# A graph layer on one core: taking 22 self-loops per step out of the gathers

## The chip, the core and the metric

The kernel runs on one core of a Trainium2 chip. The metric is the device time of one execution in microseconds. Kernels are compared by the median of several runs; a profile is one further execution, with its own time.

## What is computed

The reference is one layer of a graph network on 50000 nodes with 128 features, with a residual and a layer norm:

```python
Xs = X[src]                                   # one row per edge, 1650000 edges
m_data = Xs @ W_data.T + b_data
m_ctrl = Xs @ W_control.T + b_control
msg = jnp.where((edge_types == 0)[:, None], m_data, m_ctrl)
agg = jax.ops.segment_sum(msg, dst, num_segments=X.shape[0])
out = relu(agg + (X @ W_self.T + b_self))
x = layernorm(x + out)
```

The edges are sorted by destination. They are 800000 random pairs in both directions, and one self-loop per node (src equal to dst). The sort is stable and the loops came last, so a node's loop is the last of its about 33 edges. Each edge has a type, 0 or 1, at random.

## The kernel before

The sum over the edges comes ahead of the weights. For each node the kernel sums the source rows of its edges of type 0 and of type 1 separately, and counts both; the weights and biases are then applied to the two sums and the counts.

**Blocks, steps, chunks.** The edge list is cut into 449 blocks of 3680 edges. A block has 28 chunks of 128 edges and one chunk of 96. It is worked on in four steps of seven chunks (the fourth has the 96 as well). A step's edges end in a window of W = 36 nodes, a block's in B = 128 nodes. Ten blocks are a group, whose edge data are loaded at once.

**Gathers.** For each chunk of 128 edges, `products` (L246) issues one indirect DMA from POOL: it fetches the 128 source rows of 512 bytes by a list of indices in SBUF into a buffer y, of which there are 70. The 96 rows of the last chunk come as single-row DMAs, half from SP's queue and half from ACT's (L234), into yx.

**Products.** TensorE multiplies each chunk's rows with a one-hot matrix (L249), which sends each row to its node's column of its type, and sums a step in PSUM (acc). The one-hot matrix of a block is one compare on VectorE (L198) of the edges' columns col_g with a row of numbers that lies in PSUM (num_ps). The counts are reductions of it (L208, L213) that TensorE puts into a third part of acc (L252).

**Sums.** VectorE adds each step's acc into a ring of three tiles, sums (L260), at the place of the step's window. ACT copies what the next block shares with this one (take_over, L265). `layer` (L270 to L273) multiplies with the weights on TensorE, `moments` and `store` (L278 to L293) do the residual, the norm and the store, one block later.

**Columns.** Once per group `columns` (L155 to L165) turns destinations and types of 128 x 290 edges into columns, and takes a least and a greatest value. These go into a flag at the end: where an edge falls out of its window, a general path recomputes everything. The flag stays zero with these inputs.

**Order.** The order is written out by hand. Each engine runs its instructions in program order. The loop runs over blocks b and steps q; the one-hot matrix, the counts and the single rows are made two blocks ahead (AHEAD). The lists of indices are used as they were loaded (tile idx_g), so the first gather waits for one load only. At the start of the run POOL's iota for num (L127) stands behind the first gathers in POOL's order, and VectorE's copy of it (L130), the clearing of sums (L145 to L147) and the computation of every block's first node from first_i (base, begin; L108 to L116) follow on VectorE.

Of the kernel before, what the change touches and what calls it, by code (L numbers as in the profile page):

```python
# [11 lines left out]
F32 = mybir.dt.float32  # L12
BF16 = mybir.dt.bfloat16
# [11 lines left out]
P = 128  # L25
# [6 lines left out]
R = 7  # L32
# [5 lines left out]
C1 = C + 1  # L38
BE = C * CH + X
NBLK = -(-E // BE)  # L40
# [6 lines left out]
GC = GB * C1  # L47
AHEAD = 2


# [17 lines left out]

def straight(ctx, tc, c, x, x_t, src_t, dst_t, etype_t, src_x, dst_first, out):

# [13 lines left out]
    ohp = ctx.enter_context(tc.tile_pool(name="ohp", bufs=AHEAD + 1))  # L84
    gat = ctx.enter_context(tc.tile_pool(name="gat", bufs=70))
    stp = ctx.enter_context(tc.tile_pool(name="stp", bufs=3))
    ps = ctx.enter_context(tc.tile_pool(name="ps", bufs=4, space=bass.MemoryType.PSUM))
    ps_o = ctx.enter_context(tc.tile_pool(name="ps_o", bufs=2, space=bass.MemoryType.PSUM))

    idx_g, d_g, t_g, one_g, col_g = {}, {}, {}, {}, {}  # L90
    stats = keep.tile([P, 2, GROUPS], F32, name="stats")

    def load_edges(g):
        t = eds.tile([1, GB * X], I32, name="one_g")
        nc.sync.dma_start(t, src_x[None, g * GB * X:(g + 1) * GB * X])
        one_g[g] = t
        for name, a, of in (("idx_g", src_t, idx_g), ("d_g", dst_t, d_g), ("t_g", etype_t, t_g)):
            t = eds.tile([P, GC], I32, name=name)
            nc.sync.dma_start(t, a[:, g * GC:(g + 1) * GC])
            of[g] = t  # L100

# [26 lines left out]
                   allow_small_or_imprecise_dtypes=True)  # L128
    num_ps = keep_ps.tile([P, 2 * W], F32, name="num_ps")
    nc.vector.tensor_copy(num_ps, num)  # L130

    to_row = keep.tile([P, 2, P], BF16, name="to_row")
    nc.vector.memset(to_row, 0.0)
# [10 lines left out]
    for t in sums:  # L144
        nc.vector.memset(t, 0.0)  # L145
        nc.vector.memset(t[0:3, 2, :], 1.0)
        nc.vector.memset(t[0:2, 2, :], 0.0)  # L147

    def columns(g):

        d, t = d_g.pop(g), t_g.pop(g)
        rel = eds.tile([P, GC], F32, name="rel")
        first = begin[:, g * GB:(g + 1) * GB, :]
        rel_b, d_b = (a.rearrange("p (b c) -> p b c", c=C1) for a in (rel, d))
        nc.vector.tensor_tensor(rel_b[:, :, :C].rearrange("p b (q r) -> p b q r", r=R),  # L155
                                d_b[:, :, :C].rearrange("p b (q r) -> p b q r", r=R),
                                first[:, :, :, None].to_broadcast([P, GB, Q, R]), op=ALU.subtract)
        nc.vector.tensor_tensor(rel_b[:, :, C:], d_b[:, :, C:], first[:, :, Q - 1:], op=ALU.subtract)
        col = eds.tile([P, GC], F32, name="col_g")
        nc.vector.tensor_scalar(col, t, 0.0, float(W), op0=ALU.not_equal, op1=ALU.mult)  # L160
        nc.vector.tensor_tensor(col, col, rel, op=ALU.add)
        chk = eds.tile([P, GC], F32, name="chk")
        nc.vector.scalar_tensor_tensor(chk, d, float(DST_PAD), rel, op0=ALU.is_lt, op1=ALU.mult)
        nc.vector.tensor_reduce(stats[:, 0, g:g + 1], chk, AX.X, ALU.min)
        nc.vector.tensor_reduce(stats[:, 1, g:g + 1], chk, AX.X, ALU.max)  # L165
        col_g[g] = col

# [5 lines left out]
    def steps_of(b):  # L173
        return [q for q in range(Q) if len(chunks_of(b, q))]

    ohs, cnts, ys, accs, xws, xTs, pos, hs, mvs, sds = {}, {}, {}, {}, {}, {}, {}, {}, {}, {}

# [12 lines left out]
    def onehot(b):  # L192
        g, i = divmod(b, GB)
        if i == 0:
            columns(g)
        n = C1 if b < NBLK - 1 else RCH
        oh = ohp.tile([P, C1, 2 * W], F32, name="oh")
        nc.vector.tensor_tensor(oh[:, :n, :], col_g[g][:, i * C1:i * C1 + n, None].to_broadcast([P, n, 2 * W]),  # L198
                                num_ps[:, None, :].to_broadcast([P, n, 2 * W]), op=ALU.is_equal)
        ohs[b] = oh  # L200
# [20 lines left out]
    def single_rows(b, q):  # L221

        if q == 0:
            ys[b] = stp.tile([X, D], F32, name="yx", bufs=AHEAD + 2)
        g, i = divmod(b, GB)
        both = []
        for j, (eng, dma) in enumerate(((SP, nc.sync), (ACT, nc.scalar))):
            at = j * SHARE + q * TURN
            _, nodes = nc.values_load_multi_w_load_instructions(  # L229
                one_g[g][0:1, i * X + at:i * X + at + TURN], engines=[eng], **RANGE)  # L230
            both.append([(dma, at + k, node) for k, node in enumerate(nodes)])
        for pair in zip(*both):
            for dma, row, node in pair:
                dma.dma_start(ys[b][row:row + 1, :], x[bass.ds(node, 1), :])  # L234

    def products(b, q):
        g, i = divmod(b, GB)
        acc = ps.tile([P, 3, W], F32, name="acc")
        ks = chunks_of(b, q)
        for k in ks:  # L240
            if k == C:
                r, y = X, ys.pop(b)
            else:
                r = LAST if b == NBLK - 1 and k == RCH - 1 else P
                y = gat.tile([P, D], F32, name="y")
                nc.gpsimd.indirect_dma_start(  # L246
                    out=y[:r], out_offset=None, in_=x,
                    in_offset=bass.IndirectOffsetOnAxis(ap=idx_g[g][:r, i * C1 + k:i * C1 + k + 1], axis=0))
            nc.tensor.matmul(acc[:, :2, :].rearrange("p t w -> p (t w)"), y[:r], ohs[b][:r, k, :],  # L249
                             start=k == ks[0], stop=k == ks[-1])  # L250
        for t in range(2):
            nc.tensor.matmul(acc[:, 2, :], to_row[:, t, :], cnts[b][:, q, t * W:(t + 1) * W],  # L252
                             start=t == 0, stop=t == 1)
        accs[b, q] = acc
# [39 lines left out]

    with tc.manual_schedule():
        for b in range(AHEAD):
            onehot(b)
            counts(b)
        for b in range(3):
            window(b)  # L300
        for b in range(AHEAD):
            for q in range(Q):
                single_rows(b, q)
        for b in range(NBLK + 1):
            if b + 3 < NBLK:
                window(b + 3)
            g, i = divmod(b, GB)
            if i == GB // 2 and g + 1 < GROUPS:
                load_edges(g + 1)
            if b > 0:  # L310
                add(b - 1, steps_of(b - 1)[-1])
                if b < NBLK:
                    take_over(b)
            qs = steps_of(b)
            for q in range(Q):
                if q in qs:
                    products(b, q)
                if q == 0 and b > 0:
                    layer(b - 1)
                if q in qs[:-1]:  # L320
                    add(b, q)
                if q == 0 and b > 0:
                    moments(b - 1)
                if q == 0 and b + AHEAD < NBLK:
                    onehot(b + AHEAD)
                if q == 1 and b > 0:
                    store(b - 1)
                if b + AHEAD < NBLK - 1:
                    single_rows(b + AHEAD, q)
                if q == 1 and b + AHEAD < NBLK:  # L330
                    counts(b + AHEAD)

# [3 lines left out]
    mm = keep.tile([P, 2], F32, name="mm")  # L336
    nc.vector.tensor_reduce(mm[:, 0:1], stats[:, 0, :], AX.X, ALU.min)
    nc.vector.tensor_reduce(mm[:, 1:2], stats[:, 1, :], AX.X, ALU.max)
    bad = keep.tile([P, 2], F32, name="bad")
    nc.vector.tensor_scalar(bad[:, 0:1], mm[:, 0:1], 0.0, None, op0=ALU.is_lt)  # L340
# [6 lines left out]
    pb = ps_o.tile([B, D], F32, name="po")  # L347
    nc.tensor.matmul(pb[:2, 0:1], bad, ones, start=True, stop=True)
    both = keep.tile([2, 1], F32, name="both")
    nc.vector.tensor_copy(both, pb[:2, 0:1])  # L350
    pc = ps_o.tile([B, D], F32, name="po")
    nc.tensor.matmul(pc[:1, 0:1], both, ones[:2, 0:1], start=True, stop=True)
    nc.vector.tensor_copy(gap[:, 2:3], pc[:1, 0:1])
# [227 lines left out]
def gnn_resnorm(  # L581
# [5 lines left out]
    dst_t: bass.AP,  # L587
    etype_t: bass.AP,
    src_x: bass.AP,
    dst_first: bass.AP,  # L590
# [37 lines left out]
    with ExitStack() as own:  # L628
        straight(own, tc, c, x, x_t, src_t, dst_t, etype_t, src_x, dst_first, out)
    found = nc.values_load(bad, min_val=0, max_val=4 * P,  # L630
                           skip_runtime_bounds_check_because="a count of at most 2 * P + 2")
    with tc.If(found > 0):
# [35 lines left out]
```

## Time and profile before

| what | value |
|---|---|
| time, median of 3 runs | 15709.57 us (15708.91 to 15711.14) |
| the profiled execution: its time | 15709.39 us |
| the profiled execution: span from first to last instruction | 15707.6 us |
| granted TensorE clock | 1.000 |
| busy: POOL / TensorE / VectorE / ACT | 76% / 62% / 24% / 2% |
| bytes moved by DMA | 971.47 MB, mean 62 GB/s |
| gathers | 12555 |
| single-row DMAs | 2 x 21504 |

A row of a group names line, engine, operation, output and inputs, and how often it ran; after the bar come the busy time in us and the mean of one in ns; after the second bar the time that the engine was idle just before these instructions, and what ended most of it. "issue" is idle time in which the engine waited for nothing that the profile shows. L249 counts two matmuls per chunk[...]. A two-input operation on VectorE is called TENSOR_TENSOR or SCALAR_TENSOR_TENSOR, one with a single tensor TENSOR_SCALAR, COPY or CAST.

### The profile page before, as it was taken

What the parts mean: (1) busy time and instruction counts of PE and PEld (TensorE: products, weight loads), DVE (VectorE), ACT (ScalarE), POOL (GpSimd) and SP (SyncE); (2) the same over time, 40 slices, a digit from 0 to 9 for tenths busy, and PEclk for the clock granted to TensorE, in tenths of its full rate; (3) what the DMA queues carried; (4) which work ended last, traced back from release to release, by engine and by line L of the source; (5) the groups of instructions that cost most, each with busy time, mean ns of one, the idle gap of its engine ahead of it and who ended that gap; (6) DMA issues with size and microseconds to landing.
All of it is one profiled execution on the core that took longest, in us unless ns stands there. A gap on an engine that the chain in (4) does not pass through costs nothing.

```text
span 15707.6 us, 248219 instructions
## 1 busy us (share of the span) xinstructions
PE 9719.2 (62%) x33193; PEld 7477.1 (48%) x33194; DVE 3846.6 (24%) x5740; ACT 365.0 (2%) x903; POOL 11860.3 (76%) x12563
## 2 busy tenths in 40 slices
PE   5666666666666666666666666666666666666666
PEld 4444444444444444444444444444444444444444
DVE  3222222222222222222222222222222222222222
ACT  0000000000000000000000000000000000000000
POOL 7777777777777777777777777777777777777777
DMA  2222222222222222222222222222222222222222
GB/s 65 62 62 62 62 63 62 62 62 62 62 62 62 63 62 62 62 62 62 62 62 63 62 62 62 62 62 62 62 63 62 62 62 62 62 62 62 63 62 58
DMA packets 703530, 971.47 MB, mean 62 GB/s; under 512 B 267712, under 2 KB 500803, under 8 KB 701856
## 3 DMA queue, kind: packets, MB, share of 16 engines
q0 software_dynamic: 401760, 823.58, 20.1%
q1 hardware_dynamic: 256650, 120.61, 2.9%
q10 hardware_dynamic: 43446, 11.29, 0.3%
q14 instruction: 1397, 11.44, 0.2%
q8 instruction: 277, 4.54, 0.1%
HBM read 924.99 MB, written 29.43 MB: 61 GB/s over the span
## 4 chain that ended last, share of the span: by engine, by line
DMA 39%; issue 37%; PE 14%; POOL 8%; ACTq 2%; DVE 0%; SPq 0%; POOLq 0%; ACT 0%; DVEq 0%
DMA y<-in_x,idx_g 38%; PE acc L249 9%; POOL y L246 8%; PE po L273 2%; PE po L271 1%; DMA yx<-in_x 1%; PE po L270 1%; ACTq L234 1%; ACTq L229 0%; PE acc L252 0%; SPq L234 0%; POOLq L246 0%; SPq L229 0%; DVE sums L260 0%; DVE st L280 0%
## 5 line engine op out<-in xcount | busy, mean ns | idle before, releaser
L246 POOL DMA_INDIRECT y<-in_x,idx_g x12555 | 11859.4, 945 | 3832.3 <-issue 2666.4
L249 PE MATMUL acc<-oh,y 128*128 128x72 f32 x25110 | 8397.3, 448 | 5957.2 <-DMA y<-in_x,idx_g 5852.6
L249 PEld LDWEIGHTS acc<-oh,y 128*128 128x128 f32 x25110 | 6240.9, 314 | 7996.6 <-DMA y<-in_x,idx_g 7247.8
L260 DVE TENSOR_TENSOR sums<-acc,sums 128x108 f32 x1794 | 486.0, 271 | 10835.0 <-PE acc L252 9773.4
L208 DVE TENSOR_REDUCE cnt<-oh 128x216 bf16<-128x1512 f32 (+1 forms) x449 | 1268.5, 2825 | 0.1
L198 DVE TENSOR_TENSOR oh<-col_g,num_ps 128x2088 f32<-128x2088 f32 (+1 forms) x449 | 1030.7, 2296 | 0.0
L252 PEld LDWEIGHTS <-to_row 128*128 128x128 bf16 x3588 | 654.4, 198 | 0.0
L273 PE MATMUL po<-wmsgT,sums 128*128 128x128 f32 x1796 | 548.7, 461 | 0.0
L213 DVE TENSOR_REDUCE cnt<-oh 128x72 bf16<-128x576 f32 (+1 forms) x449 | 526.1, 1172 | 0.0
L265 ACT COPY sums<-sums 128x384 f32 x448 | 229.4, 512 | 11662.5 <-DMA yx<-in_x 11590.1
L252 PE MATMUL acc<-cnt,to_row 128*128 128x36 bf16 x3588 | 480.1, 217 | 0.0
L273 PEld LDWEIGHTS po<-wmsgT,sums 128*128 128x128 f32 x1796 | 416.3, 322 | 100.7 <-issue 100.7
L278 DVE SCALAR_TENSOR_TENSOR h<-po,xw 128x128 f32<-128x128 f32 x449 | 130.8, 291 | 949.2 <-PE po L273 949.2
L271 PE MATMUL po<-bias,sums 3*128 3x128 f32 x898 | 355.6, 497 | 9.5 <-DVE sums L260 8.2
L270 PE MATMUL po<-wselfT,xT 128*128 128x128 f32 x898 | 348.7, 492 | 0.0
L249 PE MATMUL acc<-oh,yx 96*128 96x72 f32 x896 | 284.6, 421 | 7.6 <-DMA yx<-in_x 7.6
L271 PEld LDWEIGHTS po<-bias,sums 3*128 3x128 f32 x898 | 223.3, 308 | 110.1 <-issue 110.1
L249 PEld LDWEIGHTS acc<-oh,yx 96*128 96x128 f32 x896 | 235.6, 323 | 7.8 <-DMA yx<-in_x 7.8
L270 PEld LDWEIGHTS po<-wselfT,xT 128*128 128x128 f32 x898 | 228.9, 317 | 0.0
L284 ACT ACTIVATE sd<-mv,eps 128x1 f32<-128x1 f32 x449 | 132.2, 295 | 3667.7 <-DVE mv L282 3667.7
L292 DVE TENSOR_SCALAR o<-h,mv,rstd 128x128 f32<-128x128 f32 x449 | 155.9, 347 | 16.6
L280 DVE BATCH_NORM_STATS2 st<-h 128x6 f32<-128x128 f32 x449 | 132.3, 295 | 15.3
(61 smaller groups left out, 294.9 us busy)
## 6 DMA issues: line engine op xcount, KB each, us to landing
yx<-in_x ACTq DMA_DIRECT2D x21504, 0.5 KB
yx<-in_x SPq DMA_DIRECT2D x21504, 0.5 KB
y<-in_x,idx_g POOLq DMA_INDIRECT x12555
xw<-in_x SPq DMA_DIRECT2D x449, 64.0 KB
xT<-in_x_t SPq DMA_DIRECT2D x449, 64.0 KB
out<-o SPq DMA_DIRECT2D x449, 64.0 KB
idx_g<-in_src_t SPq DMA_DIRECT2D x45, 145.0 KB
d_g<-in_dst_t SPq DMA_DIRECT2D x45, 145.0 KB
```

The lines of the kernel that those rows point to most:

```text
L198: nc.vector.tensor_tensor(oh[:, :n, :], col_g[g][:, i * C1:i * C1 + n, None].to_broadcast([P, n, 2 * W]), num_ps[:, None, :].to_broadcast( ...
L208: nc.vector.tensor_reduce(cnt[:, :n, :], ohs[b][:, :n * R, :].rearrange("p (q r) w -> p q w r", r=R), AX.X, ALU.add)
L213: nc.vector.tensor_reduce(cnt[:, q, :], ohs[b][:, k[0]:k[-1] + 1, :].rearrange("p r w -> p w r"), AX.X, ALU.add)
L234: dma.dma_start(ys[b][row:row + 1, :], x[bass.ds(node, 1), :])
L246: nc.gpsimd.indirect_dma_start(out=y[:r], out_offset=None, in_=x, in_offset=bass.IndirectOffsetOnAxis(ap=idx_g[g][:r, i * C1 + k:i * C1 + ...
L249: nc.tensor.matmul(acc[:, :2, :].rearrange("p t w -> p (t w)"), y[:r], ohs[b][:r, k, :], start=k == ks[0], stop=k == ks[-1])
L252: nc.tensor.matmul(acc[:, 2, :], to_row[:, t, :], cnts[b][:, q, t * W:(t + 1) * W], start=t == 0, stop=t == 1)
L260: nc.vector.tensor_tensor(part, accs.pop((b, q)), part, op=ALU.add)
L265: nc.scalar.copy(sums[b % RING][:, :, :B], sums[(b - 1) % RING][:, :, bass.ds(at, B)])
L270: nc.tensor.matmul(po, xTs.pop(b), c["wselfT"], start=True, stop=False)
L271: nc.tensor.matmul(po, a[0:3, 2, :B], bias, start=False, stop=False)
L273: nc.tensor.matmul(po, a[:, t, :B], c["wmsgT"][:, t * D:(t + 1) * D], start=False, stop=t == 1)
```

## The change

A step now covers 7 x 128 + 22 edges. The 22 that follow the step's own 896 (the "filling" edges) have no place of their own: in each step the first 22 self-loops among the 896 are taken out of the gather, and the 22 filling edges take their places. So a block has 3768 edges and the same 28 gathers, and there are 438 blocks, of which the last, with 27 chunks, is worked as before. What the removed loops would have added is added in another way: a loop's row is the node's own row, so the kernel counts per node and type how many loops were left out and multiplies the node's row (xT, loaded anyway) by that count.

What it needs for this:

- **Loads.** Three more loads per group: source, destination and type of the filling edges, 880 numbers each, repeated on all 128 partitions (450 KB each). They are issued from SP at the second block of a group.
- **columns**, per group: marks the loops (src equal to dst), numbers them within their step by matmuls with a triangular and a full matrix of ones (rank), does for the filling edges (128 x 880) what it did for the others (128 x 290), and packs source and column of an edge into one number (v, v_f).
- **fill**, per block, five blocks ahead (RAHEAD): compares the ranks with 0 to 21 (m, 128 x 28 x 22), multiplies and sums to get the filling edge for each place, and unpacks it into idx, the list of the gather, and into col. Another product and a strided sum (by) pick the columns of the left-out loops.
- **left_out_columns, _matrix, _numbers, _rows, add_left_out**, per block: a matmul sums by over the partitions, a compare makes a one-hot matrix z (88 x 256), three matmuls count the loops per node and type on all partitions (pl), VectorE multiplies with xT, and adds the result into sums.

The lists of numbers that fill compares and multiplies with are copied into PSUM first. The PSUM pools are divided anew: ps_o has one buffer instead of two. Before the loop fill, left_out_columns and left_out_matrix run for the first five blocks. The first gather now waits for fill of block 0, and POOL's iotas stand ahead of it in POOL's order. The flag also covers that a step has fewer than 22 loops.

```diff
-BE = C * CH + X
+F = 22
+BE = C * CH + Q * F + X
...
+RAHEAD = 5
...
+        for name, a in (("sf", src_f), ("df", dst_f), ("tf", etype_f)):
+            t = eds.tile([P, GB, Q, F], I32, name=name, bufs=1)
+            nc.sync.dma_start(t.rearrange("p b q f -> p (b q f)"),
+                              row_bcast(a[g * GB * Q * F:(g + 1) * GB * Q * F]))
...
+    def columns_of(d, t, first, name):
+        rel = eds.tile(list(d.shape), F32, name="rel" + name, bufs=1)
+        for r, a, f in first(rel, d):
+            nc.vector.tensor_tensor(r, a, f, op=ALU.subtract)
+        col = eds.tile(list(d.shape), F32, name="col" + name, bufs=1 if name else 2)
+        nc.vector.tensor_scalar(col, t, 0.0, float(W), op0=ALU.not_equal, op1=ALU.mult)
+        nc.vector.tensor_tensor(col, col, rel, op=ALU.add)
+        return col, rel
+
+    def check(d, rel, at, name):
+        chk = eds.tile(list(d.shape), F32, name="chk" + name, bufs=1)
         nc.vector.scalar_tensor_tensor(chk, d, float(DST_PAD), rel, op0=ALU.is_lt, op1=ALU.mult)
...
+    def packed(src, col, name):
+        lim = eds.tile(list(col.shape), F32, name="lim" + name, bufs=1)
+        nc.vector.tensor_scalar(lim, col, 0.0, float(P - 1), op0=ALU.max, op1=ALU.min)
+        v = eds.tile(list(col.shape), F32, name="v" + name)
+        nc.vector.scalar_tensor_tensor(v, src, float(P), lim, op0=ALU.mult, op1=ALU.add)
+        return v
...
+        h = eds.tile([P, GB, Q, R + 1], BF16, name="h_loop", bufs=1)
+        nc.vector.memset(h, 0.0)
+        nc.vector.tensor_tensor(h[:, :, :, :R], a["s"][:, :, :C].rearrange(steps, r=R),
+                                a["d"][:, :, :C].rearrange(steps, r=R), op=ALU.is_equal)
+        rank = ps_r.tile([P, GB * Q, R + 1], F32, name="rank")
+        nc.tensor.matmul(rank, below, hs_, start=True, stop=False)
+        for r in range(R):
+            nc.tensor.matmul(rank[:, :, r + 1:], ones_b, hs_[:, :, r:r + 1].to_broadcast([P, GB * Q, R - r]),
+                             start=False, stop=r == R - 1)
+        col, rel = columns_of(a["d"], a["t"], first_of, "")
+        check(a["d"], rel, [stats[:, 0, m, g:g + 1] for m in range(2)], "")
+        col_f, rel_f = columns_of(a["df"], a["tf"], first_of_f, "_f")
+        check(a["df"], rel_f, [stats[:, 1, m, g:g + 1] for m in range(2)], "_f")
+        v = packed(a["s"], col, "")
+        v_f = packed(a["sf"], col_f, "_f")
+        cb = eds.tile([P, GB, C], F32, name="cb")
+        nc.vector.tensor_scalar(cb, a["t"][:, :, :C], 0.0, float(P), op0=ALU.not_equal, op1=ALU.mult)
+        nc.vector.tensor_tensor(cb, cb, a["d"][:, :, :C], op=ALU.add)
+        nc.vector.tensor_tensor(cb, cb, base[:, g * GB:(g + 1) * GB, :].to_broadcast([P, GB, C]), op=ALU.subtract)
...
+    def fill(b):
+        g, i = divmod(b, GB)
+        if i == 0:
+            columns(g)
...
+        nc.vector.tensor_copy(vf, v_f[:, i].rearrange("p q f -> p (q f)"))
+        nc.vector.tensor_copy(cb, cb_g[g][:, i, :])
+        m = fil.tile([P, C, F], F32, name="m")
+        nc.vector.tensor_tensor(m, rk_g[g][:, i, :, None].to_broadcast([P, C, F]),
+                                rank_no_ps[:, None, :].to_broadcast([P, C, F]), op=ALU.is_equal)
+        new = fil.tile([P, C, F], F32, name="new")
...
+        nc.vector.tensor_reduce(v, new, AX.X, ALU.add)
+        nc.vector.tensor_tensor(vi, v, stay[:, i, :], op=ALU.add)
+        nc.vector.tensor_single_scalar(idx, vi, 7, op=ALU.logical_shift_right)
+        nc.vector.scalar_tensor_tensor(col_g[g][:, i, :C], idx, -float(P), vi, op0=ALU.mult, op1=ALU.add)
+        nc.vector.tensor_tensor(old, m, cb[:, :, None].to_broadcast([P, C, F]), op=ALU.mult)
+            nc.vector.tensor_reduce(by, old.rearrange("p (q r) f -> p q f r", r=R), AX.X, ALU.add)
...
+            nc.tensor.matmul(pc, bys.pop(b).rearrange("p q f -> p (q f)"), ones_b[:, 0:1], start=True, stop=True)
...
+            nc.vector.tensor_copy(at, pcs.pop(b))
+            nc.vector.tensor_scalar(z.rearrange("p t n -> p (t n)"), node_no, at, None, op0=ALU.is_equal)
...
+            nc.tensor.matmul(pl[:, :2, :].rearrange("p t n -> p (t n)"), ones_b[:Q * F, :],
+                             z.rearrange("p t n -> p (t n)"), start=True, stop=True)
+            for t in range(2):
+                nc.tensor.matmul(pl[:, 2, :], to_row[:Q * F, t, :], z[:, t, :], start=t == 0, stop=t == 1)
...
+            nc.vector.tensor_tensor(rows, rows, xTs[b][:, None, :].to_broadcast([P, 2, B]), op=ALU.mult)
...
+            nc.vector.tensor_tensor(part, pls.pop(b)[:, :, :B], part, op=ALU.add)
...
-                    in_offset=bass.IndirectOffsetOnAxis(ap=idx_g[g][:r, i * C1 + k:i * C1 + k + 1], axis=0))
+                    in_offset=bass.IndirectOffsetOnAxis(ap=idxs[b][:r, k:k + 1], axis=0))
...
+            if b < NBLK:
+                add_left_out(b)
             qs = steps_of(b)
             for q in range(Q):
                 if q in qs:
                     products(b, q)
                 if q == 0 and b > 0:
                     layer(b - 1)
+                if q == 1:
+                    left_out_numbers(b + 1)
+                if q == 3:
+                    left_out_columns(b + RAHEAD)
                 if q in qs[:-1]:
                     add(b, q)
...
+                if q == 2:
+                    left_out_rows(b + 1)
+                    if b + RAHEAD < NBLK:
+                        fill(b + RAHEAD)
+                if q == 3:
+                    left_out_matrix(b + RAHEAD)
```

## The prediction

> **What bounds the kernel now.** I read the page first: its shares of busy time and its groups of instructions.
>
> ```profile
> span 15707.6 us, 248219 instructions
> ...
> PE 9719.2 (62%) x33193; PEld 7477.1 (48%) x33194; DVE 3846.6 (24%) x5740; ACT 365.0 (2%) x903; POOL 11860.3 (76%) x12563
> ...
> L246 POOL DMA_INDIRECT y<-in_x,idx_g x12555 | 11859.4, 945 | 3832.3 <-issue 2666.4
> L249 PE MATMUL acc<-oh,y 128*128 128x72 f32 x25110 | 8397.3, 448 | 5957.2 <-DMA y<-in_x,idx_g 5852.6
> ```
>
> POOL looks only 76% busy, but its one group has 11859.4 us of work and 3832.3 us of idle time, together 15691.7 of the 15707.6 us. The idle time is not a wait for anybody: it is about 0.30 us behind each of the 12555 gathers. TensorE, for its part, idles 5957.2 us, nearly all of it for gathered rows. So the kernel is a chain of gathers on POOL.
>
> The list of all instructions of line L246 puts the first gather's start at 3.9 us and the last one's at 15692.3 us: 15688.4 us in 12554 spacings, 1.2497 us each. This mean holds some disturbed ones, which the timeline shows. Its columns are start, duration, engine, line, operation, and in brackets the idle time before it. First the start of the run:
>
> ```profile
> 20.40 2.33 POOL L246 DMA_INDIRECT y<-in_x,idx_g  x1 [0.30 <-issue]
> 20.86 0.70 DVE L145 MEMSET sums<- 128x768 f32 x1
> ...
> 22.48 1.96 DVE L112 TENSOR_TENSOR begin<-first_i,base 128x1800 f32<-128x1800 int32 x1
> 23.04 2.84 POOL L246 DMA_INDIRECT y<-in_x,idx_g  x1 [0.30 <-issue]
> ...
> 24.67 1.08 DVE L113 TENSOR_SCALAR begin<-begin 128x1800 f32<-128x1800 f32 x1
> ...
> 26.18 1.25 POOL L246 DMA_INDIRECT y<-in_x,idx_g  x1 [0.31 <-issue]
> 26.21 1.09 DVE L115 CAST place_i<-begin 1x1800 int32<-1x1800 f32 x1
> ...
> 27.54 2.01 DVE L116 TENSOR_TENSOR begin<-begin,base 128x1800 f32<-128x1800 f32 x1
> 27.73 2.64 POOL L246 DMA_INDIRECT y<-in_x,idx_g  x1 [0.30 <-issue]
> ```
>
> Four gathers took 9.06 us instead of 4 x 0.94: VectorE's work on SBUF delayed POOL by 5.3 us in the 9.1 us from 20.40. Then a group boundary, which comes once in ten blocks:
>
> ```profile
> 7998.84 0.46 DVE L161 TENSOR_TENSOR col_g<-col_g,rel 128x290 f32<-128x290 f32 x1
> 7998.97 1.15 POOL L246 DMA_INDIRECT y<-in_x,idx_g  x1 [0.30 <-issue]
> ...
> 7999.22 0.45 DVE L163 SCALAR_TENSOR_TENSOR chk<-d_g,rel 128x290 f32<-128x290 int32 x1
> ...
> 8000.44 2.32 DVE L198 TENSOR_TENSOR oh<-col_g,num_ps 128x2088 f32<-128x2088 f32 x1
> ```
>
> Here the small two-input operations cost one gather 0.21 us. L198, five times as long but with an operand in PSUM, costs none: the gather at 8000.42 lasts 0.94. Taking out 5.3 us at the start and 44 x 0.2 us at the groups leaves 15674 / 12554 = **1.2485 us per undisturbed gather**.
>
> **What is removed.** A step takes 7 x 128 + 22 edges where it took 7 x 128, so a block takes 3768 edges for the same 28 gathers. That is 438 blocks for 449, and 437 x 28 + 27 = 12263 gathers for 12555. From first to last gather: 12262 x 1.2485 = **15309.1 us**, 365 us less in spacings. The 96 single rows, the one-hot compare and the counts per block stay; there are 11 blocks fewer of them.
>
> **The start.** Before, gathers could start as soon as the first list had landed (3.9 us). Now the first one needs idx of block 0, the end of a VectorE chain. Before, that chain had waited for POOL's iota until 17.77 us (it stood behind eleven gathers); now the iota stands ahead of the gathers, and VectorE goes on at about 7.8, when the weights are through. The memsets and copies take 3.7 us (17.77 to 21.49), the new ones about 1 us: 12.5. I allow 13 for first_i (issued at 7.49, now behind three transfers of 450 KB). Base and begin take 8.1 us (21.49 to 29.55): 21. Then columns of group 0. Two-input operations go by L161 (290 elements, 463 ns) and L116 (1800, 2007 ns): 0.166 us + 1.02 ns per element, so 1.07 us for 880. Plain scalar operations go by L160 (290, 313 ns) and L113 (1800, 1079 ns): 0.61 us for 880. The 880-wide ones sum to 4 x 1.07 + 2 x 0.61 + 2 reductions of 1.07 = 7.6 us, the 290-wide ones to 5.8, the final min/max checks that slip in to 0.9, and block 0's fill up to idx to 3.2: 17.5 us, less 0.08 us of overlap at each of 33 boundaries, 15. First gather at **37 us**; I keep 32 to 46. The old start's 5.3 us of delay is gone, as that work now lies before the first gather.
>
> **VectorE, per block.** m, new and old with 616 elements: 3 x 0.80. The reduction over 22: 0.79. The strided one, by L213 (576 elements, 1173 ns): 1.25. Two copies into PSUM by L130 (0.24): 0.44. vi, idx, col: 3 x 0.17. at and z: 0.5 (L292, 347 ns). Products with xT and the addition into sums: about 1. Together 6.9 us, and per group some 14 us more of columns, 1.4 per block. VectorE had 3846.6 / 449 = 8.6 us per block, so 16.9 of the 28 x 1.2485 = 35.0 us. TensorE had 21.6 and gets about 1.4 more (rows like L252's 217 ns). Both stay well under 35, and I cost this work at nothing as time: POOL runs ahead of it. What covers it is the gather's 70 buffers, 87 us. The worst place is the group boundary: columns and fill (some 21 us) stand in VectorE's queue ahead of the reduction that TensorE's sum of by waits for behind step 3, and that step takes 10 us of gathers. TensorE waits about 11 us, and with it layer, ACT's take_over and the single rows behind it; 9 more rows lie in buffers, and TensorE works a backlog off at 0.44 us a chunk (L249 at 35.21 us: 14 matmuls, 7 chunks, in 3.23 us) against 1.25 of arrival. Without the cover it would be 43 x 11 = 473 us. The gather's own new wait is on idx, written five blocks ahead; nothing is late.
>
> **VectorE against the gathers.** This is the real price, since a delayed gather is never made good. Only operations with both inputs in SBUF, or plain single-source ones from SBUF to SBUF, showed delays. By the Trainium skill, "SBUF — State Buffer", section "Who interferes with whom", the shared port pair is a lock, held for the whole instruction, and the loser is blocked entirely. That speaks against this change: columns now holds it for 4 x 1.07 + 2 x 0.61 + 9 two-input operations of 290 or less (3.9) + 3 scalar ones (0.9), with a memset about 10.4 us per group, and by the rule taken for the sum 43 x 10.4 = 447 us would go to POOL. The rows are kinder: 1.6 us of such operations per group (L155, L160, L161, L163) cost 0.2 us, and L163, begun before the delayed gather had ended, added nothing. The gather seems to need the port at brief moments: near its start, and for single-source operations also near its end. An operation of length L then catches such a moment with chance L / 1.25 and holds it L / 2 on average: L² / 2.5. The four old ones give 0.28 us against 0.2 measured, a factor of 0.7. The new columns: 4 x 0.46 + 2 x 0.30 (two moments) + 0.68 + 0.25 = 3.4 us, times 0.7 = 2.3 us per group. Group 0 lies before the first gather: 43 x 2.3 = **99 us**. The ends are 0.2 us per group (9 us) and, by the ratio of the start, 5.3 of 9.1 us, 0.58 x 10.4 = 6.0 us (258 us). I stay near L161, whose shapes half of these have.
>
> Per block vi, idx, col and z touch SBUF alone, 0.86 us of it. The nearest row is L292, 347 ns in each block, beside which the gather's mean stays 945 ns: nothing. Ends 0 and 0.86 us; I take 0.05 us x 438 = **22 us**.
>
> **Transfers.** A group loads 1350 KB more. While first_i (900 KB) moved after 7.49 us, the gathers from 7.83 to 16.57 kept 0.94 and 0.30, so nothing is charged; were a load to hold up gathers by 3 us, it would be 130 us.
>
> **Sum.** 37 + 15309.1 + 99 + 22 + 15.3 from the last gather to the end (15692.3 to 15707.6) = 15482.4, and 1.8 us around the span (the profiled execution took 15709.39 us; the median of the runs, 15709.57, is the same within 0.2): **15484 us**, 1.4% less.
>
> **Rivals.**
> - Long port holds (10%). Back-to-back operations of 1 us act as at the start of the run, 6.0 us per group: 15385 + 258 = 15643 us. For: the four gathers shown. Against: those operations were twice as long.
> - Slower than before (5%). The lock passes on everything: VectorE's columns hold POOL for all their 10.4 us, 15385 + 447 = 15832 us. The point from which it decides is (15709.4 - 15385) / 43 = 7.5 us per group. Against it stands the gather at 7998.97, which slipped through between L161 and L163.
> - The loop of VectorE and TensorE becomes the pace (3%): 16.9 us of VectorE plus waits for TensorE in one block. It would have to exceed 35.0 us; at 36 it is 437 x 36 = 15732 and the start, 15800 us. Against: VectorE waits 10.8 ms for TensorE now.
> - The change doesn't hold (2%): a step with under 22 loops would set the flag and run the general path, 400 x 35 gathers more, over 17 ms. A count in the inputs gives 24 to 31 loops per step, so the flag should stay zero.
>
> The main case has 80%, from 15367 (start at 32, 0.2 us per group, nothing per block) to 15566 (start at 46, 4 us per group). To leave out no more than 2 in 10 and to take in the dearer end of the groups, the range reaches to the first rival: 15370 to 15645. A measurement of this kernel can tell about 0.2%, 31 us, from no change. Faster by more 0.91, within it 0.03, slower 0.06.
>
> **What would show it.** Right: 12263 gathers at a mean near 945 to 955 ns, first start near 37 us, spacing about 1.249 outside the group boundaries, VectorE near 45% busy, delays of some 2 us in each group at rel_f to v_f. Wrong: gathers waiting for TensorE (buffers full) or for VectorE (idx), a spacing that is longer in every block, or delays of over 4 us per group.

## The result, and the profile after

The changed kernel takes **15434.24 us** (median of 4 runs, 15433.9 to 15435.49) against 15709.24 us of the kernel before beside it (15708.39 to 15711.14): ratio 0.9825, 95% interval 0.9808 to 0.9842. The prediction was 15484, 50 us more.

The page's rows after, for those shown of before:

```profile
span 15432.5 us, 254222 instructions
...
PE 9551.6 (62%) x34515; PEld 7418.5 (48%) x34516; DVE 7169.3 (46%) x12518; ACT 355.9 (2%) x881; POOL 11631.9 (75%) x12273
...
L408 POOL DMA_INDIRECT y<-in_x,idx x12236 | 11605.0, 948 | 3760.9 <-DMA y<-in_x,idx 1973.1
```

VectorE's busy time is nearly double (3846.6 to 7169.3 us), POOL's went down by 228 us. POOL is still the whole length of the run: the group's 11605.0 + 3760.9 us, and the last 27 gathers, which use the list s and form a group of their own. The page names a DMA as what ended most of the idle time; it is the same pause of 0.30 us behind each gather as before. The only long POOL waits lie before the first gather: 11.0 us of the iota and 28.2 us for idx.

From the list of all gathers I split each span in the same way: start of the first gather, number of spacings by the mean of the undisturbed ones (those under 1.275 us), what the longer ones have above that mean (delays), and the time from the start of the last gather to the end.

| us | before | predicted | after |
|---|---|---|---|
| first gather starts | 3.9 | 37 | 41.7 |
| spacings | 12554 x 1.2485 | 12262 x 1.2485 = 15309.1 | 12262 x 1.2486 = 15310.6 |
| delays of gathers | 14.3 | 99 + 22 | 59.8 |
| last gather to end | 15.3 | 15.3 | 20.5 |

Against the prediction: +4.7 +1.5 -61.2 +5.2, which is -50.

A group boundary of after, on the timeline (start, duration, engine, line, operation, in brackets the idle time before it):

```profile
248.71 1.06 DVE L188 TENSOR_TENSOR rel_f<-df,begin 128x880 f32<-128x880 int32 x1
249.44 1.15 POOL L408 DMA_INDIRECT y<-in_x,idx  x1 [0.30 <-DMA y<-in_x,idx]
249.69 0.61 DVE L190 TENSOR_SCALAR col_f<-tf 128x880 f32<-128x880 int32 x1
250.34 1.08 DVE L191 TENSOR_TENSOR col_f<-col_f,rel_f 128x880 f32<-128x880 f32 x1
...
250.89 1.33 POOL L408 DMA_INDIRECT y<-in_x,idx  x1 [0.30 <-DMA y<-in_x,idx]
251.33 1.07 DVE L196 SCALAR_TENSOR_TENSOR chk_f<-df,rel_f 128x880 f32<-128x880 int32 x1
...
252.53 0.94 POOL L408 DMA_INDIRECT y<-in_x,idx  x1 [0.30 <-issue]
...
264.87 0.23 PE L299 MATMUL small<-ones_b,by 128*88 128x1 bf16 x1 [9.93 <-DVE by L292]
...
264.97 3.23 PE L411 MATMUL acc<-oh,y 128*128 128x72 f32 x14
```

The gather of 249.44 is 0.21 us over its 0.94, the one of 250.89 is 0.39 over. Both delays fit one rule: a two-input operation that already runs when the gather starts, and still runs 0.13 us later, holds the gather to the operation's end (rel_f ends at 249.77, col_f at 251.42). I counted over the whole run the gathers that have such an operation on SBUF alone at 0.13 us, with at least 0.06 us of it to come. In 171 of them the operation had begun 0.06 us or more before the gather. All 171 were held, by 326 ns on the mean, and the operations' rest was 324. In 146 the operation began less than 0.03 us before the gather or after the gather's start, with a rest of 115 ns: none was held. Of the 36 in between 2 were. The 171 delays make 55.8 of the 59.8 us. col_f's scalar operation, 0.61 us, fell between two gathers' starts and cost nothing; chk_f too, since the gather that col_f had just released is followed by the next one only at 252.53, when chk_f is over. TensorE waited 9.93 us for by, while the gathers went on, and then worked off seven chunks in 3.23 us.

### The profile page after: what moved, and what is told of

It is laid out like the page before. It is cut to its first block, busy times and chain, and to the rows that moved or that the text cites. A ratio compares the mean times of both kernels' runs of the same rounds, so it can differ in the third digit from the quotient of the medians.

```text
span 15432.5 us, 254222 instructions
## 1 busy us (share of the span) xinstructions
PE 9551.6 (62%) x34515; PEld 7418.5 (48%) x34516; DVE 7169.3 (46%) x12518; ACT 355.9 (2%) x881; POOL 11631.9 (75%) x12273
## 4 chain that ended last, share of the span: by engine, by line
DMA 69%; issue 11%; POOL 10%; PE 7%; DVE 2%; POOLq 0%; SPq 0%; ACTq 0%; DVEq 0%; ACT 0%
DMA y<-in_x,idx 68%; POOL y L408 10%; PE acc L411 4%; PE po L435 1%; PE po L433 1%; PE po L432 0%; POOLq L408 0%; DMA yx<-in_x 0%; SPq L396 0%; ACTq L396 0%; DVE by L292 0%; PE acc L414 0%; DMA y<-in_x,s 0%; DVE stats L198 0%; DVE stats L199 0%
## 5 line engine op out<-in xcount | busy, mean ns | idle before, releaser
L408 POOL DMA_INDIRECT y<-in_x,idx x12236 | 11605.0, 948 | 3760.9 <-DMA y<-in_x,idx 1973.1
L411 PE MATMUL acc<-oh,y 128*128 128x72 f32 x24526 | 8011.2, 446 | 5293.3 <-DMA y<-in_x,idx 5204.0
L370 DVE TENSOR_REDUCE cnt<-oh 128x216 bf16<-128x1512 f32 x438 | 1238.3, 2827 | 0.1
L360 DVE TENSOR_TENSOR oh<-col,small 128x2088 f32<-128x2088 f32 x438 | 1005.8, 2296 | 0.0
L292 DVE TENSOR_REDUCE by<-old 128x88 bf16<-128x616 f32 x437 | 583.2, 1335 | 15.1
L375 DVE TENSOR_REDUCE cnt<-oh 128x72 bf16<-128x576 f32 x438 | 512.7, 1170 | 0.0
L276 DVE TENSOR_TENSOR new<-m,small 128x616 f32<-128x616 f32 x437 | 347.5, 795 | 14.9
L273 DVE TENSOR_TENSOR m<-rk,small 128x616 f32<-128x616 f32 x437 | 347.5, 795 | 14.8
L280 DVE TENSOR_REDUCE v_new<-new 128x28 f32<-128x616 f32 x437 | 347.3, 795 | 14.9
L289 DVE TENSOR_TENSOR old<-m,small 128x616 f32<-128x616 f32 x437 | 343.5, 786 | 0.1
```

Of the source, the lines that this page charges most:

```text
L273: nc.vector.tensor_tensor(m, rk_g[g][:, i, :, None].to_broadcast([P, C, F]), rank_no_ps[:, None, :].to_broadcast([P, C, F]), op=ALU.is_equal)
L276: nc.vector.tensor_tensor(new.rearrange("p (q r) f -> p q r f", r=R), m.rearrange("p (q r) f -> p q r f", r=R), vf.rearrange("p (q f) -> p ...
L292: nc.vector.tensor_reduce(by, old.rearrange("p (q r) f -> p q f r", r=R), AX.X, ALU.add)
L360: nc.vector.tensor_tensor(oh[:, :n, :], col_g[g][:, i, :n, None].to_broadcast([P, n, 2 * W]), num_ps[:, None, :].to_broadcast([P, n, 2 * W ...
L370: nc.vector.tensor_reduce(cnt[:, :n, :], ohs[b][:, :n * R, :].rearrange("p (q r) w -> p q w r", r=R), AX.X, ALU.add)
L375: nc.vector.tensor_reduce(cnt[:, q, :], ohs[b][:, k[0]:k[-1] + 1, :].rearrange("p r w -> p w r"), AX.X, ALU.add)
```

## The experiments

**The question.** The theory: additions cost POOL time only where an operation of VectorE that works on SBUF alone covers a brief moment of a gather; the rest of the new work is hidden, by POOL's lead and 70 buffers. The rivals: such operations hold POOL for their whole length; VectorE's time itself, or the waits at the group boundary, cost something; the end and the start make the difference.

The interval of a ratio is some 26 us to either side. Differences smaller than that are read from the split of the traces and from the spread of the runs, not from the ratios.

### A chip with slower single rows: short, f12, noadd, bufs6

Four kernels ran on one chip on which the kernel before itself took 23218.81 us. Their times say little of the theory, for there another path was the bound. No other runs were made on that chip, so whether it or something at that time was the cause stays open.

short is the kernel before, ended where it has as many gathers as the changed one; it leaves out the last 37000 or so edges and their nodes:

```diff
-NBLK = -(-E // BE)
-REST = E - (NBLK - 1) * BE
+USED = 437 * BE + 3384
+NBLK = -(-USED // BE)
+REST = USED - (NBLK - 1) * BE
...
-    nc.vector.memset(base[:, NBLK - 1:, :], float(N - B))
```

> The kernel before, stopped after 437 blocks and one of 27 chunks; the last 37000 edges and their nodes are left out. It has the changed kernel's 12263 gathers and none of its additions. The gather-chain theory: 3.9 + 5.3 (start) + 12262 x 1.2485 + 44 x 0.2 + 15.3 + 1.8 = 15344 us, so that the additions cost the changed kernel 90 us, all in its start, its groups and its end. If fewer gathers were not what shortened the time, it would stay well above 15434.

f12 is the changed kernel with `F = 12` for `F = 22`.

> 12 loops per step instead of 22: 443 blocks and 12394 gathers, with everything that the change adds, only narrower (480 filling edges per group for 880). Gather chain with short holds of the port: first gather about 38.5, 12393 x 1.2486 = 15473.9, 44 groups x 0.8, end 20.5, 1.7 around: 15570 us. If the additions had a fixed price per block beside the gathers, it would come out higher by that price less 12/22 of it.

noadd is the changed kernel without by, left_out_* and add_left_out; it leaves out what the removed loops would have added:

```diff
-        nc.vector.tensor_tensor(old, m, cb[:, :, None].to_broadcast([P, C, F]), op=ALU.mult)
...
-            nc.vector.tensor_reduce(by, old.rearrange("p (q r) f -> p q f r", r=R), AX.X, ALU.add)
...
-            if b < NBLK:
-                add_left_out(b)
...
-                    left_out_matrix(b + RAHEAD)
```

> The loops are taken out and the filling edges put in, but the loops' rows are not added back (old, by, the sums, z, pl and the addition into sums are left out), so the output lacks them. The theory that this work is covered by the gathers: 15434 within 10 us, though VectorE loses some 4 us per block and TensorE the wait at the group boundary. The theory that VectorE's work leaks into the gathers per block: 50 to 400 us less.

bufs6 is the changed kernel with six buffers for y:

```diff
-    gat = ctx.enter_context(tc.tile_pool(name="gat", bufs=70))
+    gat = ctx.enter_context(tc.tile_pool(name="gat", bufs=6))
```

> 6 buffers for gathered rows instead of 70. Theory: at a group boundary TensorE stands still for 9.9 us while 7 to 8 more gathers go out, so about 10 buffers are in use; with 6, POOL waits some 5 us per group, 43 x 5 = 215 us: 15650. If the ordinary distance from issue to product needs more than 6 buffers, much more. The rival, that the wait never reached POOL: 15434.

Measured: short 22682.00 us (ratio to the kernel before 0.9771, 0.9755 to 0.9787), f12 22636.38 (0.9750, 0.9734 to 0.9767), noadd 22782.84 (0.9813, 0.9797 to 0.9829), bufs6 22158.74 (0.9545, 0.9529 to 0.9561). All four expectations missed. What held short, by its waits (engine and output, what it waited for, us in all, times, longest):

```profile
ACT sums L265 <- DMA yx<-in_x: 21711.0, 434, 197.8
DVE sums L260 <- ACT sums L265: 18754.9, 436, 58.0
PE acc L249 <- DMA yx<-in_x: 14176.3, 432, 59.2
...
POOL y L246 <- PE acc L249: 6100.2, 1417, 19.8
```

TensorE waits 14.2 ms for the single rows, about 33 us in each block; POOL waits 6.1 ms for TensorE, that is for free buffers. In f12, noadd and bufs6 too ACT's wait for the single rows is the longest, 16.3 to 21.3 ms. SP's and ACT's issues follow each other at 1.06 and 0.95 us on the mean (spacings under 5 us), in the kernel before on the first chip at 0.57 and 0.51. An undisturbed gather kept its spacing of 1.248 us. Where the single rows are the bound, a block costs what its 96 rows cost: 438 / 449 = 0.9755, near short's ratio. The differences among the four don't follow the number of blocks, and I can't explain them. short and bufs6 were run again below; f12 and noadd were not, so what less filling would give stays untried.

### What the additions cost in all: short2

short2 is short again, on a chip where the kernel before took 15709.12 us.

> The kernel before, stopped after 437 blocks and one of 27 chunks; the last 37000 edges and their nodes are left out. It has the changed kernel's 12263 gathers and none of its additions. The gather-chain theory: 3.9 + 5.3 (start) + 12262 x 1.2485 + 44 x 0.2 + 15.3 + 1.8 = 15344 us, so that the additions cost the changed kernel 90 us, all in its start, its groups and its end. If fewer gathers were not what shortened the time, it would stay above 15434.

Measured: **15349.55 us** (15348.71 to 15349.85).

```profile
L246 POOL DMA_INDIRECT y<-in_x,idx_g x12263 | 11583.5, 945 | 3743.0 <-issue 2511.5
```

These are 12263 gathers, as many as after has, with the old start and no additions. So the fewer gathers alone give 359.6 us, and the additions take back 84.7: first gather at 41.67 instead of 3.85 us, 37.8; delays 59.8 instead of 13.7, 46.1; about 1 from the spacing. Its end is 20.4 us, like after's: the longer end isn't the additions' doing.

### Moments or whole holds: tt4 and tr4

Both are the changed kernel with four more operations of 128 x 880 on VectorE in each block, behind the counts, whose result nothing uses: with two inputs in SBUF (tt4), or with one, a reduction (tr4).

```diff
+                    for _ in range(4):
+                        nc.vector.tensor_tensor(wide[2], wide[0], wide[1], op=ALU.add)
```

> Four added two-input operations of 880 elements in SBUF per block (about 1.07 us each, result unused). Moments theory: each delays a gather only if it lies over the moment at which the gather reads, 0.2 to 0.46 us each on average, 4 x 437 of them: 350 to 800 us more, 15780 to 16230. Whole-hold theory: 4 x 1.07 x 437 = 1870 more, 17300. No contention: 15434.

```diff
+                    for _ in range(4):
+                        nc.vector.tensor_reduce(least_w, wide[0], AX.X, ALU.min)
```

> Four added reductions of 880 elements per block in the same place, the same 1.07 us each, with one input. If only the port matters: 15434 within 10. If VectorE's time itself leaks into the gathers, it goes up like the run with two inputs.

Measured: tt4 15853.98 us (15851.79 to 15858.79), tr4 15440.69 (15439.28 to 15444.40). From tt4's page, the engines and the gathers:

```profile
PE 9583.0 (60%) x34515; PEld 7422.1 (47%) x34516; DVE 8985.4 (57%) x14265; ACT 356.1 (2%) x881; POOL 12055.2 (76%) x12273
...
L412 POOL DMA_INDIRECT y<-in_x,idx x12236 | 12028.2, 983 | 3759.6 <-issue 2380.6
```

and from tr4's:

```profile
PE 9547.1 (62%) x34515; PEld 7415.4 (48%) x34516; DVE 8967.7 (58%) x14265; ACT 356.3 (2%) x881; POOL 11641.3 (75%) x12273
...
L412 POOL DMA_INDIRECT y<-in_x,idx x12236 | 11614.3, 949 | 3759.5 <-issue 2425.1
```

VectorE is as busy in one as in the other, 1.8 ms above after. The reductions cost 6.5 us, of which 2.3 are a later first gather (the clearing of the new tiles): VectorE's time is free here. The two-input operations cost 420 us. The delays are 476.8 us against 59.8, 0.96 us in each of the 436 blocks that have them, of the 4.4 us that they run. tt4's timeline shows why not all of it:

```profile
8000.48 4.40 DVE L509 TENSOR_TENSOR wide<-wide,wide 128x880 f32<-128x880 f32 x4
8001.40 0.95 POOL L412 DMA_INDIRECT y<-in_x,idx  x1 [0.30 <-issue]
...
8002.66 0.94 POOL L412 DMA_INDIRECT y<-in_x,idx  x1 [0.31 <-PE acc L415]
...
8003.91 1.78 POOL L412 DMA_INDIRECT y<-in_x,idx  x1 [0.31 <-issue]
```

Three gathers begin under the four operations, and one is delayed. The last two operations singly:

```profile
8002.68 1.08 DVE L509 TENSOR_TENSOR wide<-wide,wide 128x880 f32<-128x880 f32 x1
...
8003.80 1.07 DVE L509 TENSOR_TENSOR wide<-wide,wide 128x880 f32<-128x880 f32 x1
```

The third began 0.02 us after the gather of 8002.66 and cost it nothing, though it ran through all the rest of it. The fourth began 0.11 us before the gather of 8003.91 and held it to its own end at 8004.87. The whole run shows the same: all 754 gathers whose operation had begun 0.06 us or more before them were held (607 ns longer, the rest 604). Of 568 whose operation began less than 0.03 us before them, or after their start, with 858 ns of it still to come on the mean, 2 were held. In return, one of these four operations that begins between 0.05 us before a gather's start and 0.03 us after it takes 1.08 to 1.15 us, where the others take 1.075. So by these counts the one that comes first has its turn, if the gather is taken to come some 0.05 us before its recorded start; and the gather's turn is short.

For a whole hold the cost would have been 436 x 4.4 us = 1918 us. The moments stand, but the deciding one lies at the gather's start: an operation that begins just after it costs nothing, however long it is.

### What covers the wait at the group boundary: bufs6b

bufs6b is bufs6 again, on a chip where the kernel before took 15709.68 us.

> 6 buffers for gathered rows instead of 70, again. Theory: at a group boundary TensorE stands still for 9.9 us while 7 to 8 more gathers go out, so about 10 buffers are in use; with 6, POOL waits some 5 us per group, 43 x 5 = 215 us: 15650. If the ordinary distance from issue to product needs more than 6 buffers, much more. The rival, that the wait never reached POOL: 15434.

Measured: **15714.41 us** (15709.58 to 15718.52, 12 runs), ratio to the kernel before 1.0003 (0.9994 to 1.0012), 280 us above after. POOL's waits for TensorE in after,

```profile
POOL y L408 <- PE acc L411: 227.2, 745, 0.3
```

and in bufs6b:

```profile
POOL y L408 <- PE acc L411: 844.9, 1894, 24.6
```

In after each of the 745 is the usual 0.3 us. In bufs6b 1894 x 0.30 = 568 us are that, and 277 us are waits. The delays grew by the same 277 us (59.8 to 336.4): 233 within 45 us of a group's columns, 5.4 for each of 43 boundaries where 5 were expected; 24 at the start of the loop, and some 20 elsewhere, which had not been reckoned. So the changed kernel with six buffers is no faster than the kernel before with its 70; the kernel before with six was not run. What covers VectorE's columns are the further buffers.

### The widths of the operations: split

split is the changed kernel with each 880-wide operation of columns in five pieces of 176:

```diff
+    def parts(name):
+        n = 2 if name else GB
+        return [slice(i, i + n) for i in range(0, GB, n)]
...
-        nc.vector.tensor_tensor(col, col, rel, op=ALU.add)
+        for s in parts(name):
+            nc.vector.tensor_tensor(col[:, s], col[:, s], rel[:, s], op=ALU.add)
```

and likewise for the other five. 

> The 880-wide two-input and scalar operations of a group in five pieces of 176 each, the same numbers. Moments theory: short pieces lie over a moment with a smaller product of chance and length, the 1.36 us of delay per group fall to about 1.0, 15 us less: 15419. Whole-hold theory: each piece has its own fixed 0.17 us, the hold grows from 10.4 to some 14.5 us per group, so the delay grows by two fifths: 15458.

Measured: 15424.57 us (15408.54 to 15429.32), 10 under after where 15 were expected. In the profiled execution the delays are 49.0 us against 59.8. But one group cost 3.57 us, more than any of after (2.13): seven gathers took 3.77 us each. And the runs lie 21 us apart where after's lie within 2. Short pieces don't always help.

### Start and end: start

start is the changed kernel with a third buffer for the weights, so that the third load needn't wait for the first two; POOL instead of VectorE clears the sums; and the flag's products lie in ps_l, so that they needn't wait for ps_o's single buffer:

```diff
-        nc.vector.memset(t, 0.0)
+        nc.gpsimd.memset(t, 0.0)
...
-    pb = ps_o.tile([B, D], F32, name="po")
+    pb = ps_l.tile([P, 3, P], F32, name="pl")[:, 0, :]
...
-    with tc.tile_pool(name="wts", bufs=2) as wts, \
+    with tc.tile_pool(name="wts", bufs=3) as wts, \
```

> The changed kernel with three buffers for the weights (so that the third is not queued behind the edge loads), the clearing of sums on POOL before its first gather, and the flag's product in another PSUM bank than the last layer's. First gather at about 32 us instead of 41.7, end 15.5 us after the last gather's start instead of 20.5: 15434 - 9.7 - 5 = 15420. If the first gather's place did not count, 15429.

Measured: 15430.64 us (15430.04 to 15432.66), 3.6 below after and 11 above what was expected. The first gather came at 37.95 us, the delays were 62.8 us, the end took 16.84. In after the start looks so:

```profile
11.90 0.45 PE L808 MATMUL pw<-ident,w_sb 128*128 128x128 f32 x1 [7.41 <-DMA w_sb<-in_L_gnn_W_self]
12.38 0.33 SPq L125 DMA_DIRECT2D first_i<-in_dst_first  x1
...
12.42 0.20 POOL L146 IOTA num<- 128x72 f32 x1 [11.02 <-PE pw L808]
...
16.81 0.40 DVE L127 TENSOR_SCALAR base<-first_i 128x440 f32<-128x440 int32 x1
```

and in start:

```profile
7.88 0.33 SPq L125 DMA_DIRECT2D first_i<-in_dst_first  x1
...
13.30 0.55 DVE L127 TENSOR_SCALAR base<-first_i 128x440 f32<-128x440 int32 x1 [3.21 <-DMA first_i<-in_dst_first]
```

The third weight load no longer holds everything back, and first_i is issued 4.5 us earlier, but then base waits 3.21 us for it. That wait is what took the place of the one removed. Of the end: POOL reads the flag 4.46 us after the start of the last gather, in after 7.27, and the end came 3.6 us sooner.

### A faster version: best, then best2

best puts it all together: 23 loops per step, the edits of split and start, and first_i loaded ahead of the weights (shown here: what start and split don't have).

```diff
-F = 22
+F = 23
...
+    first_i = const.tile([P, TBL, Q], I32, name="first_i")
+    nc.sync.dma_start(first_i.rearrange("p b q -> p (b q)"), row_bcast(dst_first))
```

> Together: 23 loops per step (14 gathers fewer), the wide operations in pieces, the start and flag edits, and first_i loaded first, ahead of the edges. From the runs so far: 15434.2 - 14 x 1.2486 (17.5) - 10.8 (shorter delays per group) - 7.4 (first gather and end) - 4 (first_i no longer behind 1320 KB) = 15395 us. If the delays of the groups don't add up with the rest: 15405.

Measured: 15445.99 us (15443.89 to 15451.65), 51 above what was expected and slower than after. The first gather came at 35.4 us and the end took 16.3, as wanted; there are 12249 gathers. The loss is in the delays, 97.3 us. best's timeline at a group boundary:

```profile
1298.32 0.91 DVE L194 TENSOR_SCALAR col_f<-tf 128x184 f32<-128x184 int32 x5
...
1298.74 3.90 POOL L418 DMA_INDIRECT y<-in_x,idx  x1 [0.30 <-DMA y<-in_x,idx]
1299.13 1.39 DVE L196 TENSOR_TENSOR col_f<-col_f,rel_f 128x184 f32<-128x184 f32 x5
...
1300.43 1.39 DVE L202 SCALAR_TENSOR_TENSOR chk_f<-df,rel_f 128x184 f32<-128x184 int32 x5
1301.86 1.11 DVE L204 TENSOR_REDUCE stats<-chk_f 128x1 f32<-128x920 f32 x1
```

One gather was held for 2.96 us, through some dozen short operations in a row, to the end of chk_f's last piece. Between the pieces it didn't get its turn. They overlap: five of 0.35 us take 1.39 us, so each begins 0.09 us before the one before it has ended. tt4's four stand 0.03 us apart, and the gathers that the first of them held were let go at its end. But col_f and chk_f in after overlap by 0.09 us as well, and there the gather was let go. There are 38 gathers of over 2 us in best and 7 in split. Why pieces of 184 elements do this in most groups and those of 176 seldom, no run here settles.

best2 is best without the pieces. 

> 23 loops per step (14 gathers fewer), the start and flag edits, first_i loaded first, and the wide operations whole again. If the run with pieces was slow by the chains of pieces alone: 15434.2 - 17.5 (gathers) - 6.3 (first gather) - 4.1 (end) = 15406 us. If the 23rd loop or the loading order was what cost it 50 us: 15440 or more.

Measured: **15415.19 us** (15414.97 to 15415.43), ratio to the kernel before 0.9813 (0.9796 to 0.9829), 19 us under after and 31 under best. First gather at 34.1, 12248 x 1.2486, delays 70.3 (the wide operations have 920 elements now), end 16.3. Its four runs lie within 0.5 us of each other and after's within 1.6, so it is the fastest, though the intervals of the two ratios overlap. The time is 9 us above what was expected: the delays are 10.5 above after's, and the first gather came 1.3 earlier than reckoned.

## Why the prediction was right, point by point

- **Fewer gathers, 1.2485 us each: right.** 12262 spacings took 15310.6 us for 15309.1, and short2 shows the gain of the count alone: 359.6 us, where the prediction had 365 less in spacings, 5.1 of which the longer end of short2 gives back.
- **VectorE and TensorE at nothing: right.** VectorE is 46% busy (predicted: about 45%); tr4 adds 1.8 ms to it for 6.5 us. No gather in the loop waits for idx.
- **The group boundary: right.** TensorE waits 9.93 us where 11 were reckoned, and bufs6b shows that with six buffers it costs 233 us, most of the gain.
- **VectorE against the gathers: right in kind, too high in size.** "99 us" was 43 groups x 2.3; it is 43 x 1.38 and 0.3 for group 0. Three terms of it failed.
  - Scalar operations were given a second moment near the gather's end. In after, 42 gathers have a scalar operation of L204 over the time 0.13 us before their end, and are 943 ns long on the mean, so there is none.
  - The chance of a hit was taken as L / 1.25. But an operation must cover the time from some 0.05 us before the gather's start to 0.13 us after it, so that 0.18 us of L don't count. With (L - 0.18)² / 2.5 the four wide operations give 0.32 us each for 0.46, the nine narrow ones 0.03 for 0.08, the two scalar ones 0.07; that is an estimate of 1.7 us per group, near the 1.38 measured.
  - Operations were taken to meet the gathers at random. A gather that was held starts its next spacing at the end of the operation that held it, so the following operation, shorter than 1.25 us, is over when the next gather starts. This follows from the rows shown (chk_f after col_f), and no run varied it alone.

  The rule of the Trainium skill, "SBUF — State Buffer", section "Who interferes with whom", taken as the prediction took it (all the time of the operations is lost to POOL), would have given 447 us where 59 were found, and 1.9 ms in tt4 where 0.42 were. What failed is that sum more than the lock: a gather that is held is held to the operation's end, and POOL loses nothing while it isn't waiting. The section also says that an operation with two inputs in SBUF contends with an instruction of GpSimd that reads SBUF; a short read by the gather at its start would fit what was measured, but no run here shows what the gather does at that moment. best comes closest to the dear case, with overlapping operations in a row. (The first rival's 5.3 of 9.1 us divides by the gathers' own durations; the stretch from 20.40 is 10.0 us long, which makes 5.5 us per group of its 6.0.)
- **Per block 22 us: nothing was found.** The undisturbed spacing is 1.2486 and all the delays but a few lie at group boundaries. That was the lower end, nothing, of what was allowed. vi, idx and col take 0.18 to 0.19 us each in after, hardly more than the 0.18 that an operation must cover to hold a gather.
- **The start at 37 us: 4.7 too early.** The failing step is "VectorE goes on at about 7.8, when the weights are through", along with "nothing is charged" for transfers. The third weight load waited behind the edge loads of the first group, 1320 KB, and TensorE transposed it at 11.90 instead of 7.01 us. base began at 16.81, begin was done at 24.61 (21 predicted), and columns and fill then took 17 us to the first gather (15 predicted; 21 and 15 are 36, where the prediction wrote 37).
- **The end at 15.3 us: 5.2 too early.** It was taken over from a run whose last block has 11 chunks; with 27 chunks it is 20.4 us without any of the additions (short2). start shows that a part hangs on when the flag is read: 2.8 us sooner, the end 3.6 us sooner. Of the 5.2 us, 1.7 are the later read of the flag (7.27 us after the last gather's start for 5.54), and 2.1 a longer drain of POOL's queue at the very end (6.02 us for 3.90, in short2 too). Why that grew, no run here shows.

So the time came out 50 us under the forecast, since 61 us of delays that were reckoned did not come, and 10 us at the two ends were not reckoned. The two errors have opposite signs, so the total is nearer than its terms.

## What to carry to other kernels

Where one engine issues transfers back to back, count those. Work that replaces them on other engines was free here, as a lead in buffers covered its longest pause; that lead has to be measured, for with six buffers instead of 70 the changed kernel was no faster than the kernel before. What such work cost the issuing engine wasn't its length but how often it was already running when a transfer began. Test this with a copy of the suspected operation beside a kind that doesn't disturb (tt4 and tr4), before cutting operations to pieces, which made best slower. And terms at the ends, of a start whose loads now queue behind others or an end with another last block, are read anew from the changed order.

## What the runs showed of the hardware that was not expected

- A gather is held by a two-input operation of VectorE on SBUF if that began some 0.05 us or more before the gather and still runs 0.13 us after the gather's start, and then to the operation's end: 0.21 us by one of 0.46, 0.39 by one of 1.08, and 0.84 by the last of tt4's four of 1.08. One that begins later doesn't hold it (566 of 568 in tt4, with 0.86 us still to run).
- A row of short, overlapping operations on SBUF alone held one gather for 2.96 us, through all their ends (best).
- On one chip the single-row transfers followed each other at about 1.0 us on the mean instead of 0.5, and the kernel before took 23219 us for 15709, while the gathers of 128 rows kept their 1.248 us.
- A weight load behind 1320 KB of other loads was 6.4 us from issue to use (5.49 to 11.90).
